# Two attention layers on one core: the first element's third item takes its denominators over memory and is scaled at the end; the projection's two blocks leave PSUM in one copy

## The chip, the core and the metric

One core of a Trainium2 chip runs the whole program. Its engines run side by side, each through its own queue in order: TensorE (PE; PEld is its loading of weights), VectorE (DVE), ScalarE (ACT), GpSimd (POOL), and SyncE (SP), which here only issues transfers. TensorE writes to PSUM, eight banks of 512 fp32 values in each of 128 partitions; ScalarE and VectorE read them from there. The metric is the device time of one execution in microseconds; the time given is the median of three runs.

## The reference

The input `x` has 16 elements (images) of 256 channels and 32 x 32 positions, all in fp32. Two layers follow each other. In the first, on the positions of an element as rows:

```
qkv  = x @ w_proj + b_proj                  # 4 heads of 64: q, k, v
attn = softmax(q @ k.T * 64**-0.5)
res  = attn @ v
x1   = res @ w_out + b_out + x
```

In the second, with a group norm `gn` over 32 groups of 8 channels:

```
q, k, v = gn(x1) @ qkv_w.T                  # 8 heads of 32
attn = softmax(q @ k.T * 32**-0.5 + phys_bias)
x2   = x1 + (attn @ v) @ proj_w.T + proj_b
out  = x2 + mlp_w2 @ gelu(mlp_w1 @ gn(x2) + mlp_b1) + mlp_b2
```

## The kernel before

**Layout.** Channels lie on the 128 partitions in `CC` = 2 chunks, the `S` = 1024 positions of an element in the free dimension, in `NT` = 2 blocks `t` of `TB` = 512. An element goes through two attentions, `attention_a` (first layer) and `attention_b` (second layer), and then the two-layer perceptron `mlp`. The elements `b` are run one after the other, but pieces of the perceptron of element b - 1 and of the query, key and value products of element b + 1 are put between the steps of an attention. The order of the program is written out by hand: the attentions are generators, a step being one block of keys (or two), and `later.after(n, fn)` runs `fn` n steps on. `tc.keep_in_program_order` and `tc.issue_after` set the order on one engine: what is traced inside `issue_after(ins)` stands behind `ins` in the queue of `ins`'s engine. Otherwise a scheduler orders the instructions of each engine when the program is built.

**The first attention.** `attention_a` works on four items, (t, c), two heads each. For each block `kb` of 128 keys the scores go to two PSUM banks (L434), ScalarE takes the exponential of the 128 x 1024 tile (L444), and `weigh` multiplies by the values (L457) and lets VectorE add the exponentials up over `kb` in `sums` (L471). At an item's last block the result leaves PSUM in two halves (L477, L478). The denominator of the softmax is the sum over keys: small matmuls with ones give it, repeated over the partitions (`den`). It is inverted in one of two ways. `denominators` (L375) copies it from PSUM (L376), lets SP spread the distinct values over all partitions (L381), inverts 16 values in each partition (L387), writes these to memory (L398) and reads them back repeated over the partitions (L403); GpSimd adds the values to two running totals from which the kernel later sees whether all denominators were in range. `normalise` does this for both items of a `t`, and `scale` multiplies. In element 0, for t = 1, `normalise_item` (L489) takes the other way: each item's denominator is inverted at full width on VectorE (L504, 128 x 512), the result multiplied (L505), and the range is kept with two reductions (L417). For item 2 (c = 0) ScalarE copies the denominator to SBUF first (L502) and this is done two steps after its end; for item 3 the reciprocal reads PSUM directly.

Behind the attention's last step stands the projection `o`: `project(0, res)` gives `first_half`, which is issued in two blocks of output channels, at L562 and L564; the part for t = 1 follows two steps after item 3. Two `o` blocks use PSUM banks `b0` and `b1`, and the two of the next `t` use the same.

**The second attention and its projection.** `attention_b` has four heads to a chunk and two blocks of keys to a step: scores (L602) into two single banks and three two-bank tiles, exponentials (L615), sums (L630), the values (L656). In elements 1 to 14 (`by_fold`) the sums of an item are folded to half height in a tile `packed_b`, kept in `spare["home"]`. When t = 0 is scaled, its projection `j` is issued in the course of the last item: `out_proj.issue` writes both blocks of 128 output channels to one two-bank tile `both` (L774), since `apart` is false there, and finds `home`. Then `leave(co)` runs for each block: ScalarE copies it to a quarter of `home` that is no longer needed and adds the bias on the way (L781), and one step later `add_up` adds it to the input and takes the statistics for the group norm on VectorE (L795, L796), behind the sums of that step. All other projections leave PSUM by one addition on VectorE that takes bias and input in (L787), with the statistics behind it (L790). The two banks of `both` are then taken by a score tile of the same step.

Of the kernel before, what the change touches and what calls it, by code (L numbers as in the profile page):

```python
# [10 lines left out]
AF = mybir.ActivationFunctionType  # L11
ALU = mybir.AluOpType
# [7 lines left out]
TB = 512  # L20
# [239 lines left out]
def first_pass(ctx, tc, x, out, k):  # L260
    nc = tc.nc
    B, C, S = x.shape
    CC, SB, NT = C // P, S // P, S // TB
    HC = k["m1b"].shape[1]
    later = Later()
# [44 lines left out]
    def wide(name, n=None):  # L310
        if n is None:
            n = next(m for m in order if m not in kept)
        use(n)
        return ps_s.tile([P, 2, TB], F32, tag=f"s{n}", name=name)

    def bank(name, n):
        return ps_a.tile([P, TB], F32, tag=f"b{n}", name=name)
# [36 lines left out]
    def product(o, w, r, **flags):  # L354
        for c0 in range(0, P, cols[0]):
            sl = slice(c0, c0 + cols[0])
            nc.tensor.matmul(o[sl], w[:, sl], r, **flags)  # L357
# [15 lines left out]
    spread_out, spare, trailing = {}, {}, []  # L373

    def denominators(key, den, d, full, waits, then, parts=1):  # L375
        nc.scalar.copy(d, den)  # L376
        n = full.shape[1]
        w = 4 * TB // P
        spread = work.tile([P, w], F32, tag="spread", name=f"sp_{key}", bufs=2)
        row = dram.tile([4 * TB // n, n], F32, tag="row", name=f"row_{key}", bufs=4)  # L380
        nc.sync.dma_start(  # L381
            spread, d[:: 32 // parts].rearrange("p (a b) -> p a b", b=w)
        )

        def invert():
            inverse = work.tile([P, w], F32, tag="inverse", name=f"inv_{key}", bufs=2)
            tc.keep_in_program_order(nc.vector.reciprocal(inverse, spread))  # L387
            if parts > 1:
                num = P // parts
                for r in range(parts):  # L390
                    nc.sync.dma_start(
                        row[:, r * n // parts : (r + 1) * n // parts].rearrange(
                            "g (a b) -> g a b", b=w
                        ),
                        inverse[r * num : (r + 1) * num],
                    )
            else:
                nc.sync.dma_start(row.rearrange("r (a b) -> (r a) b", b=w), inverse)  # L398
            nc.gpsimd.tensor_add(dsum, dsum, spread)
            nc.gpsimd.tensor_add(isum, isum, inverse)  # L400
            num = P * n // (4 * TB)
            for r in range(P // num):
                spread_out["last"] = nc.sync.dma_start(  # L403
                    full[r * num : (r + 1) * num], row[r].partition_broadcast(num)
                )
            later.after(waits[1], lambda: then(full))

        later.after(waits[0], invert)
# [5 lines left out]
    def add_to_range(den, inverse):  # L414
        for tot, what in ((dsum, den), (isum, inverse)):
            part = small.tile([P, 1], F32, tag="part", name="part")
            nc.vector.tensor_reduce(part, what, AX.X, ALU.add)  # L417
            nc.gpsimd.tensor_add(tot[:, :1], tot[:, :1], part)

    def attention_a(b, qT, kT, v, project):  # L420
        key, D, lag = f"a_{b}", D0, 2
        items = [(t, c) for t in range(NT) for c in range(CC)]
        units = [(i, kb) for i in range(len(items)) for kb in range(SB)]
        res = act.tile([P, CC, S], F32, tag="res", name=f"res_{key}")
        accs, held, sums, both, pair, homes = {}, {}, {}, {}, [], []
# [63 lines left out]
        def normalise_item(i):  # L489
            t, c = items[i]  # L490
            den = wide(f"den_{key}_{i}", next(m for m in order if m != 2))[:, 0, :]
            for j in range(4):
                nc.tensor.matmul(
                    den[j * 32 : (j + 1) * 32, :], k["ones"], sums[i][:, j // 2, :],
                    start=True, stop=True,
                )
            if not c:
                homes.append(act.tile([P, CC, S], F32, tag="k1", name=f"d_{key}_{t}"))
            full, held_den = homes[0][:, c, :TB], homes[0][:, c, TB:]
            r = res[:, c, t * TB : (t + 1) * TB]  # L500
            if c < CC - 1:
                nc.scalar.copy(held_den, den)  # L502
                den = held_den
            tc.keep_in_program_order(nc.vector.reciprocal(full, den))  # L504
            tc.keep_in_program_order(nc.vector.tensor_mul(r, r, full))  # L505
            if c == CC - 1:
                later.after(2, lambda: project(t, res)())
            later.after(3, lambda: add_to_range(den, full))

        def normalise(t):  # L510
            half = TB // 2
# [44 lines left out]
        while pending:  # L556
            weigh(*pending.pop(0))
            if not pending:


                first_half = project(0, res)
                first_half((0,), True)  # L562
                yield
                first_half((1,), True)  # L564
                cols[0] = P
                break
            yield
# [199 lines left out]
    def out_proj(key, w, src, bias, xs, t, stats, then):  # L767
        todo = list(range(CC))

        def issue(cos=range(CC), apart=False):  # L770
            home = None if apart else spare.pop("home", None)
            apart = apart or cols[0] == P
            if not apart:
                both = wide(f"{key}_{t}")  # L774
            ps = {}

            def leave(co):
                y = xs[:, co, t * TB : (t + 1) * TB]
                if home is not None:
                    held = home[:, 2 + co]  # L780
                    nc.scalar.activation(  # L781
                        held, ps[co], AF.Identity, bias=bias[:, co : co + 1]
                    )
                    later.after(1, lambda: add_up(co, y, held))
                    return
                else:
                    nc.vector.scalar_tensor_tensor(  # L787
                        y, ps[co], bias[:, co : co + 1], y, ALU.add, ALU.add
                    )
                nc.vector.bn_stats(stats[:, co, t, :], y)  # L790
                todo.remove(co)

            def add_up(co, y, held):
                with tc.issue_after(spread_out["es"].ins):
                    nc.vector.tensor_add(y, y, held)  # L795
                    nc.vector.bn_stats(stats[:, co, t, :], y)  # L796

            def part(co, kc):
                product(
                    ps[co],  # L800
                    w[:, kc, co * P : (co + 1) * P],
                    src(kc),
                    start=(kc == 0),
                    stop=(kc == CC - 1),
                )

            for co in cos:
                ps[co] = bank(f"{key}_{t}_{co}", co) if apart else both[:, co, :]
            if apart:
                for co in cos:  # L810
                    for kc in range(CC):
                        part(co, kc)
                    leave(co)
            else:
                for kc in range(CC):
                    for co in cos:
                        part(co, kc)
                for co in cos:
                    leave(co)
            if not todo and then:  # L820
                then()

        return issue
# [208 lines left out]
    def input_sums(key, y):  # L1032
        sums = weights_tile(f"qk7t_{key}")
        b11, b12 = (y[:, 0, t * TB : (t + 1) * TB] for t in range(NT))
        b21, b22 = (y[:, 1, t * TB : (t + 1) * TB] for t in range(NT))
        t1, t2, t3, t4 = (sums[:, n] for n in range(4))
        nc.vector.tensor_sub(t3, b22, b12)
        nc.vector.tensor_sub(t1, b12, b11)
        nc.vector.tensor_sub(t2, b22, t1)
        nc.vector.tensor_sub(t4, b21, t2)  # L1040
        return dict(t1=t1, t2=t2, t3=t3, t4=t4, b11=b11, b21=b21, b22=b22)
# [295 lines left out]
    ps, n = bank("bqk", 0), brow.shape[0]  # L1337
# [44 lines left out]
    for b in range(B):  # L1382
        def load_next(b=b):
# [3 lines left out]
            with tc.issue_after(spread_out["last"].ins):  # L1387
                load_blocks(1, b - 1)
                if b + 1 < B:
# [9 lines left out]
                lambda st, b=b, xn=xn, seven=seven, sums_1=sums_1: group_norm(  # L1399
                    f"g{b}", xs[b], st, k["g1w"], k["g1b"], "res", xn, 2 if b else 1,  # L1400
                    (lambda y: sums_1.update(input_sums(f"b{b}", y))) if seven else None,
                ),
# [62 lines left out]
        if first:  # L1465
# [10 lines left out]
                lambda st, b=b, hn=hn: group_norm(  # L1476
                    f"h{b}", xs[b], st, k["g2w"], k["g2b"], "q1", hn,
                    *((3 if b + 1 < B else 1), lambda y, b=b: sums_of_input(b, y)),
                ),
# [305 lines left out]
```

## Time and profile before

| | us |
|---|---|
| median of three runs | 3605.08 |
| lowest and highest | 3604.25, 3606.47 |
| the profiled execution | 3603.56 |
| its span, first to last instruction | 3601.8 |
| granted TensorE clock | 1.0 of full |

| group | count | mean ns | busy us |
|---|---|---|---|
| L504 full-width reciprocal, items 2 and 3 of element 0 | 2 | 3352 | 6.7 |
| L781 ScalarE copy with bias, 128 x 512 | 28 | 683 | 17.7 |
| L444 exponential, 128 x 1024 | 512 | 1024 | 520.7 |
| L795 VectorE addition, 128 x 512 | 28 | 682 | 19.1 |
| L787 addition with bias from PSUM, 128 x 512 | 100 | 744 | 74.2 |

A line of the profile names engine, source line, operation and tiles (written <- read). In a timeline the first two numbers are start and duration in microseconds, x is the number of instructions merged, and the bracket gives the idle time before them and what ended it. In a list of waits the three numbers are the total, how often, and the longest. Shares of busy time are averages; what a change is worth is read at the place where it works. Matmuls packed into parts of the array run side by side, so their number and duration say less than the distance from one group's start to the next.

### The profile page before, as it was taken

The numbers are of one execution on the slowest core, as the hardware profiler recorded it, in microseconds if no ns is written. First come the engines' busy times: TensorE is split into PE (matmuls) and PEld (weight loads), VectorE is DVE, ScalarE is ACT, GpSimd is POOL, SyncE is SP. The second block draws the span as 40 slices with busy tenths as digits, with TensorE's granted clock in tenths as the row PEclk, the third lists the DMA queues.
The fourth block names the chain that finished last, engine by engine and source line by source line (L and its number), as shares of the span: only waits on it lengthen the run. The fifth ranks groups of instructions, "written<-read, shape, count | busy, mean of one in ns | idle before, by whom it ended". The sixth has DMA issues, their size and how long they took to land.

```text
span 3601.8 us, 81991 instructions
## 1 busy us (share of the span) xinstructions
PE 3584.2 (100%) x35705; PEld 1470.2 (41%) x35705; DVE 2786.2 (77%) x3187; ACT 2283.0 (63%) x3196; POOL 219.1 (6%) x319
## 2 busy tenths in 40 slices
PE   9999999999999999999999999999999999999999
PEld 3334344343444434444344443434434444343433
DVE  5786877868788687876868878688786977868777
ACT  4665757667475675856658566585665757657572
POOL 4000100001000010000000000000000000000000
PEclk9999999999999999999999999999999999999999
DMA  3011311213122131221312213121121212213100
GB/s 130 8 57 33 78 54 38 74 38 83 45 43 69 39 81 45 50 64 36 81 45 52 66 33 81 45 55 63 39 76 45 55 63 47 74 39 64 51 28 28
DMA packets 81137, 197.78 MB, mean 55 GB/s; under 512 B 37666, under 2 KB 38434, under 8 KB 74626
## 3 DMA queue, kind: packets, MB, share of 16 engines
q1 hardware_dynamic: 71392, 163.85, 14.9%
q0 software_dynamic: 7632, 28.21, 5.1%
q8 instruction: 282, 4.62, 0.5%
q14 instruction: 85, 0.70, 0.1%
q10 hardware_dynamic: 1746, 0.40, 0.1%
HBM read 125.32 MB, written 22.27 MB: 41 GB/s over the span
## 4 chain that ended last, share of the span: by engine, by line
PE 92%; DVE 4%; issue 2%; DMA 1%; SPq 1%; ACT 1%; DVEq 0%; POOL 0%
PE s_b L602 12%; PE s_a L434 12%; PE acc_a L457 12%; PE acc_b L656 11%; PE m L357 10%; PE m L1146 10%; PE qk_b L1052 4%; PE qk_a L1052 3%; PE v_b L357 3%; PE j L357 3%; PE v_a L357 3%; PE o L357 3%; PE qk7y_b L1052 1%; PE qk7y_a L1052 1%; DVE es_b L630 1%
## 5 line engine op out<-in xcount | busy, mean ns | idle before, releaser
L615 ACT ACTIVATE e_b<-s_b 128x1024 f32<-128x1024 f32 (+1 forms) x1280 | 981.8, 865 | 135.6 <-PE s_b L602 135.6
L630 DVE TENSOR_TENSOR es_b<-es_b,e_b 128x2048 f32<-128x2048 f32 (+1 forms) x460 | 881.5, 1934 | 104.7 <-ACT e_b L615 88.3
L444 ACT ACTIVATE e_a<-s_a 128x1024 f32<-128x1024 f32 x512 | 520.7, 1024 | 360.3 <-PE s_a L434 359.6
L434 PE MATMUL s_a<-q,k 64*64 64x512 f32 x4096 | 544.5, 593 | 0.7 <-DVE res_a L478 0.7
L457 PE MATMUL acc_a<-e_a,v 64*64 64x512 f32 x4096 | 540.3, 589 | 0.0
L602 PE MATMUL s_b<-q,k 32*64 32x512 f32 x8192 | 527.1, 600 | 2.7 <-ACT v L928 1.3
L471 DVE TENSOR_TENSOR es_a<-es_a,e_a 128x1024 f32<-128x1024 f32 x384 | 469.8, 1224 | 66.0 <-ACT e_a L444 46.5
L656 PE MATMUL acc_b<-e_b,v 128*32 128x512 f32 x4096 | 492.2, 598 | 0.0
L357 PE MATMUL m<-g,w 128*32 128x256 f32 (+2 forms) x6464 | 416.6, 385 | 0.0
L357 PEld LDWEIGHTS m<-g,w 128*32 128x32 f32 (+1 forms) x6464 | 224.7, 111 | 212.0 <-issue 61.8
L457 PEld LDWEIGHTS acc_a<-e_a,v 64*64 64x64 f32 x4096 | 188.2, 133 | 251.2 <-issue 214.9
L602 PEld LDWEIGHTS s_b<-q,k 32*64 32x64 f32 x8192 | 175.9, 130 | 251.0 <-issue 133.0
L434 PEld LDWEIGHTS s_a<-q,k 64*64 64x64 f32 x4096 | 176.0, 133 | 247.5 <-issue 208.1
L656 PEld LDWEIGHTS acc_b<-e_b,v 128*32 128x32 f32 x4096 | 108.5, 109 | 351.5 <-ACT e_b L615 194.7
L630 DVE TENSOR_TENSOR es_b<-e_b,e_b 128x2048 f32<-128x2048 f32 (+1 forms) x72 | 147.0, 2051 | 131.2 <-ACT e_b L615 131.2
L1146 PE MATMUL m<-gn_h,w 128*128 128x512 f32 x512 | 242.5, 602 | 2.7 <-DVE x L1267 1.3
L1210 DVE TENSOR_TENSOR g<-g,g 128x512 f32<-128x512 f32 (+1 forms) x185 | 195.5, 1067 | 1.2 <-PE m L357 0.8
L1146 PE MATMUL m<-hs,w 128*128 128x512 f32 x384 | 178.2, 593 | 0.1
L1161 ACT ACTIVATE g<-g,m1b 128x512 f32<-128x512 f32 x128 | 91.8, 720 | 112.4 <-DVE g L1190 84.5
L1146 PEld LDWEIGHTS m<-gn_h,w 128*128 128x128 f32 x512 | 93.1, 190 | 118.7 <-issue 100.0
L1161 ACT ACTIVATE g<-m,m1b 128x512 f32<-128x512 f32 x128 | 80.9, 683 | 79.0 <-PE m L1146 79.0
L357 PE MATMUL v_a<-wp,x 128*32 128x256 f32 (+1 forms) x1952 | 121.7, 379 | 0.0
(225 smaller groups left out, 3527.9 us busy)
## 6 DMA issues: line engine op xcount, KB each, us to landing
w<-w_kept SPq DMA_DIRECT2D x30, 1792.0 KB
packed_b<-es_b SPq DMA_DIRECT2D x42, 512.0 KB
packed_b<-es_b POOLq DMA_DIRECT2D x42, 512.0 KB, 6.2
rd_b<-row_b SPq DMA_DIRECT2D x252, 64.0 KB
out_dram<-x SPq DMA_DIRECT2D x63, 256.0 KB
d_a<-row_a SPq DMA_DIRECT2D x62, 256.0 KB
x<-in_x_dram SPq DMA_DIRECT2D x30, 512.0 KB
qk<-qk_kept SPq DMA_DIRECT2D x14, 1024.0 KB
```

Source lines behind the costliest of these rows:

```text
L357: nc.tensor.matmul(o[sl], w[:, sl], r, **flags)
L434: nc.tensor.matmul(s[h : h + HALF, g, :], kT[g * D : (g + 1) * D, c, kb * P + h : kb * P + h + HALF], qT[g * D : (g + 1) * D, c, t * TB : ...
L444: nc.scalar.activation(e, s, AF.Exp, scale=float(D) ** -0.5)
L457: nc.tensor.matmul(accs[i][h][g * D : (g + 1) * D, :], v[h * HALF : (h + 1) * HALF, kb, c * 2 + g], e[h * HALF : (h + 1) * HALF, g, :], st ...
L471: spread_out["es"] = nc.vector.tensor_add(sums[i], held[i] if kb == 1 else sums[i], e)
L602: nc.tensor.matmul(outs[g][h : h + HALF, :], kT[g * D : (g + 1) * D, c, k0 : k0 + HALF], qT[g * D : (g + 1) * D, c, t * TB : (t + 1) * TB] ...
L615: spread_out["exp"] = nc.scalar.activation(to, s, AF.Exp, scale=float(D) ** -0.5)
L630: ins = nc.vector.tensor_add(d, (d if kb else es[0][:, g : g + step]), es[m][:, g : g + step])
L656: nc.tensor.matmul(acc[g * D : (g + 1) * D, :], v[:, kb + m, c * G + g], es[m][:, g, :], start=(m == 0), stop=(m == 1),)
L1052: nc.tensor.matmul(to, w, x[right], start=first, stop=True, skip_group_check=not first)
L1146: nc.tensor.matmul(ps, blocks[1][number - 1][:, i * P : (i + 1) * P], inputs[b][number], start=first, stop=True, skip_group_check=not first,)
L1210: (nc.vector.tensor_add if plus else nc.vector.tensor_sub)(d, d, more)
```

## The change

Part one concerns element 0, t = 1. Item 2 no longer gets its full-width reciprocal: `normalise_item` calls `denominators`, which takes the same trip over memory as the other blocks, into `homes[0][:, 0, :TB]`, and its product isn't taken there. The product moves to item 3's call, where the loop first multiplies item 2 by its inverse, then takes item 3's reciprocal and multiplies that. The last product is kept as `spread_out["scaled"]`; the VectorE instructions of `first_half` and of the reductions for item 3's range are put behind it. The range of item 2 goes the way of `denominators`, by GpSimd.

Part two concerns the projection `j` of t = 0 in elements 1 to 14. ScalarE takes both blocks from PSUM in one copy of 128 x 1024 without the bias, and `add_up` now does what `leave` does elsewhere, for both blocks: an addition on VectorE that takes in bias and input, and the statistics. Its inputs lie in SBUF.

In the compiled program TensorE issues the same matmuls; in element 0 one query-and-key matmul for element 1 stands before the second half of `o` instead of behind it, and one that stood behind the second statistics matmul stands before it. From element 1 on no engine's order changes but for the replaced instructions, and SP has six transfers more in element 0.

```diff
             full, held_den = homes[0][:, c, :TB], homes[0][:, c, TB:]
-            r = res[:, c, t * TB : (t + 1) * TB]
             if c < CC - 1:
-                nc.scalar.copy(held_den, den)
-                den = held_den
-            tc.keep_in_program_order(nc.vector.reciprocal(full, den))
-            tc.keep_in_program_order(nc.vector.tensor_mul(r, r, full))
-            if c == CC - 1:
-                later.after(2, lambda: project(t, res)())
-            later.after(3, lambda: add_to_range(den, full))
+                denominators(f"{key}_{i}", den, held_den, full, (2, 3), lambda full: None)
+                return
+            for m in range(CC):
+                r = res[:, m, t * TB : (t + 1) * TB]
+                if m == c:
+                    tc.keep_in_program_order(nc.vector.reciprocal(full, den))
+                scaled = tc.keep_in_program_order(
+                    nc.vector.tensor_mul(r, r, homes[0][:, m, :TB])
+                )
+            spread_out["scaled"] = scaled
+            later.after(2, lambda: project(t, res)())
+
+            def to_range():
+                with tc.issue_after(scaled.ins):
+                    add_to_range(den, full)
+
+            later.after(3, to_range)
...
                 first_half = project(0, res)
-                first_half((0,), True)
+
+                def part(co):
+                    if b:
+                        return first_half((co,), True)
+                    with tc.issue_after(spread_out["scaled"].ins):
+                        first_half((co,), True)
+
+                part(0)
                 yield
-                first_half((1,), True)
+                part(1)
...
-            def leave(co):
+            def leave(co, held=None):
                 y = xs[:, co, t * TB : (t + 1) * TB]
-                if home is not None:
-                    held = home[:, 2 + co]
-                    nc.scalar.activation(
-                        held, ps[co], AF.Identity, bias=bias[:, co : co + 1]
-                    )
-                    later.after(1, lambda: add_up(co, y, held))
-                    return
-                else:
-                    nc.vector.scalar_tensor_tensor(
-                        y, ps[co], bias[:, co : co + 1], y, ALU.add, ALU.add
-                    )
+                nc.vector.scalar_tensor_tensor(
+                    y, ps[co] if held is None else held[:, co], bias[:, co : co + 1], y,
+                    ALU.add, ALU.add,
+                )
                 nc.vector.bn_stats(stats[:, co, t, :], y)
-                todo.remove(co)
-
-            def add_up(co, y, held):
+                if held is None:
+                    todo.remove(co)
+
+            def add_up(held):
                 with tc.issue_after(spread_out["es"].ins):
-                    nc.vector.tensor_add(y, y, held)
-                    nc.vector.bn_stats(stats[:, co, t, :], y)
+                    for co in range(CC):
+                        leave(co, held)
...
-                for co in cos:
-                    leave(co)
+                if home is not None:
+                    held = home[:, 2:4]
+                    nc.scalar.copy(held, both)
+                    later.after(1, lambda: add_up(held))
+                else:
+                    for co in cos:
+                        leave(co)
```

## The prediction

> **What bounds the kernel now.** I read the page's busy times first, then TensorE's waits, then timelines of the places that the change touches. Busy times and waits:
>
> ```profile
> span 3601.8 us, 81991 instructions
> PE 3584.2 (100%) x35705; PEld 1470.2 (41%) x35705; DVE 2786.2 (77%) x3187; ACT 2283.0 (63%) x3196; POOL 219.1 (6%) x319
> ...
> PE den_a L493 <- DVE es_a L471: 2.6, 1, 2.6
> PE o L357 <- DVE res_a L541: 1.5, 2, 0.8
> PE warm L345 <- DVE nothing L1330: 1.5, 1, 1.5
> ```
>
> TensorE is idle for only 3601.8 - 3584.2 = 17.6 us in the whole span, so only what shortens a wait of TensorE can shorten the kernel, and no more than those waits. The longest one happens once: `den_a` of L493 stands 2.6 us behind VectorE's sums. It belongs to the first element's last item. VectorE's timeline there:
>
> ```profile
> 76.44 1.22 DVE L471 TENSOR_TENSOR es_a<-es_a,e_a 128x1024 f32<-128x1024 f32 x1
> 77.57 3.35 DVE L504 RECIPROCAL d_a<-d_a 128x512 f32<-128x512 f32 x1
> 80.83 1.16 DVE L471 TENSOR_TENSOR es_a<-es_a,e_a 128x1024 f32<-128x1024 f32 x1
> 81.91 0.68 DVE L505 TENSOR_TENSOR res_a<-res_a,d_a 128x512 f32<-128x512 f32 x1
> 82.51 1.27 DVE L417 TENSOR_REDUCE part<-d_a 128x1 f32<-128x512 f32 x2
> 83.69 5.20 DVE L471 TENSOR_TENSOR es_a<-es_a,e_a 128x1024 f32<-128x1024 f32 x4
> 88.82 0.68 DVE L478 TENSOR_TENSOR res_a<-res_a,acc_a 128x512 f32<-128x512 f32 x1
> 90.17 3.36 DVE L504 RECIPROCAL d_a<-den_a 128x512 f32<-128x512 f32 x1 [0.67 <-PE den_a L493]
> ```
>
> A full-width reciprocal (3.35 us), a product and two reductions of item 2 sit among the sums of item 3, and the sums end at 88.89, though their last exponential ended at 84.98 (ScalarE: 83.96 plus 1.02).
>
> A busy TensorE can also hide a loss, since packed matmuls can run half filled. In each element from 1 to 14 there is one such place, after `j`, the projection of the second attention:
>
> ```profile
> 414.90 1.98 PE L602 MATMUL s_b<-q,k 32*64 32x512 f32 x32
> 416.80 1.92 PE L656 MATMUL acc_b<-e_b,v 128*32 128x512 f32 x16
> 418.54 3.67 PE L357 MATMUL j<-res_b,wpj 128*32 128x512 f32 x32
> 422.15 2.54 PE L602 MATMUL s_b<-q,k 32*64 32x512 f32 x32
> 424.62 1.93 PE L656 MATMUL acc_b<-e_b,v 128*32 128x512 f32 x16
> ```
>
> The same 32 matmuls take 416.80 - 414.90 = 1.90 us up to the next group before `j`, and 424.62 - 422.15 = 2.47 us after it: 0.57 us lost with no idle time shown. I compared all starts of this block: the 0.57 is there in all 14 elements. ScalarE and the tile's own view say why:
>
> ```profile
> 422.29 1.26 ACT L781 ACTIVATE packed_b<-j,pjb 128x512 f32<-128x512 f32 x2 [1.96 <-PE j L357]
> 423.44 3.83 ACT L615 ACTIVATE e_b<-s_b 128x512 f32<-128x512 f32 x5
> ...
> who waited for it (us, times):
>   PEld s_b L602: 0.4, 1
> ```
>
> The last score tile of the block takes the two PSUM banks that `j` occupied. ScalarE frees them with its second copy, which ends at 423.551; the last eight matmuls start at 423.604.
>
> **What the Trainium skill says.** "Advanced Engine Details and Errata", The Read-Write Bubble: the latency of the memories shows between instructions, and "TRN2 allows reading multiple PSUM banks with single instruction". The trace agrees: L444 reads 1024 wide in 1024 ns, while two 512-wide L781 take 1.26 us. "VectorE: DVE Perf Modes", The TRN2 errata, gives ScalarE reading PSUM 172 cycles plus one for each element at 1.2 GHz: an estimate of 997 ns for 1024 elements and 570 for 512; the trace has 582 for the 512-wide copy of L477. "TensorE: Matmul & The Clock Gate", The mechanism, calls matmuls strictly first in, first out. This trace doesn't agree for packed ones: each fp32 matmul runs twice. In an undisturbed block eight tiles start their first passes within 50 ns and their second passes 0.48 us later, while at 157.92 us one tile ran both passes (157.917 and 158.396) before the seven behind it, held up, began at 159.062. "DMA: Bandwidth & Descriptors", Anatomy of one DMA, puts the fixed cost of a transfer at about 2 us, mostly the receipt of the write. The trace has 1.39 us for a row written and 2.05 for it read back, at 150.25 and 153.00.
>
> **Part one, element 0, item 2.** Removed from VectorE before the last sums: reciprocal 80.83 - 77.57 = 3.26, product 81.91 to 82.51 = 0.60, two reductions 82.51 to 83.69 = 1.18, together 5.04 us. Added: one 128x16 reciprocal (L387, 0.25). The sums then follow the exponentials, whose ends are 78.12, 79.89, 81.55, 83.33 and 84.98; a sum starts some 0.05 us after its exponential and takes 1.22, so the last ends at 86.25. TensorE's own work before `den_a` allows a start at about 86.4 (89.05 less the 2.58 of idle, less the change of shape). VectorE's end plus the 0.13 us seen before (88.89 to 89.02) gives 86.4 too. So the wait goes: **-2.6 us**.
>
> New is a round trip through memory. ScalarE's copy ends at 77.18 as before. SP spreads it (0.70) and it lands 2.0 us after the copy's end (in item 0: 60.99 to 63.07), at 79.25. The small reciprocal stands on VectorE behind the second sum (to 79.4) and ends near 79.65, before the third sum's exponential at 79.89, so it delays nothing. The row's write, SP's four issues and the landing took 150.22 to 155.05 = 4.83 us in the same form in the second attention, so `d_a` lands at 84.5. SP has nothing else between 67.3 and 142.3 us, and its queue runs empty there. GpSimd's two additions replace two others of about 0.2 to 0.7 us, with nothing behind them until 103.
>
> The product of item 2 moves behind the last L478. It waits for `d_a` at the head of VectorE's in-order queue, and behind it stand the last reciprocal, its product and the evacuation of both `o` banks, for which the second half of `o` waits. L478 ends at 87.9 (ScalarE's copy ends at 87.12). With `d_a` there at 84.5 there are 3.4 us to spare. Then: product to 88.5, reciprocal to 91.8, product to 92.4, first evacuation of `o` to 93.0. The compiled order gives TensorE, from 86.4: `den_a` 0.86, `o` 3.57, then three key-and-query matmuls instead of two: 2.57 plus the changes of shape, to 93.5. So the delayed evacuations are hidden by that third matmul with 0.4 us to spare; the statistics end at about 99.3 against 99.5 of TensorE. After the second statistics matmul one matmul less is left as cover: three are 2.6 us, and normalisation delivered its first block 2.54 us after it before. Cost nothing, up to 0.3 if either margin is off. Bounds: -2.7 to -1.3.
>
> **Part two, elements 1 to 14.** Two 512-wide copies become one of 1024. The trace has no such copy; L444's exponential of that shape takes 1024 ns, the page's estimate is 997, L615's back-to-back ones 1046. I take 1.02. It starts at 422.29 as before, because the first copy already waited for all of `j`. It ends at 423.31 instead of 423.55, the eight matmuls start 0.24 earlier, and so does all that follows: 14 x 0.24 = **-3.4 us**. If these matmuls had to queue behind the other tiles' second passes (423.488 to 423.508), only 0.10 to 0.12 would be gained, 14 x 0.11 = -1.6. If the whole gap closed, -8.0.
>
> VectorE's two additions (682 ns) become additions with a bias. Rows of that operation with one input in PSUM stand at 742 to 748; with both in SBUF there is none. I take 0.74, between 0.68 (nothing) and 1.4 (two passes). At 0.06 x 2 it adds 0.12 us an element. Behind them stands L674, which ends at 434.32 and frees the bank that `acc_a` takes at 435.57; 1.25 us cover it, 1.0 after TensorE's advance. Cost nothing. Nothing is late next in the element: `den_b` at 431.97 needs sums that ended at 430.6.
>
> **Sum.** -2.6 - 3.4 = -6.0 us on the profiled execution's 3603.56 (its span is 3601.8, 1.8 lie around it) gives 3597.6. The median of the runs shown is 3605.08, 1.5 above it; on that scale **3599.1 us**, 0.17% less. A measurement of this kernel can tell about 0.2% (7.2 us) from no change, so the forecast lies just inside that bound.
>
> **Rivals.**
> The eight matmuls queue in order, or the copy takes 1.1 us or more: -2.6 - 1.6 = -4.2, 3600.9. For it the skill's FIFO sentence; against it the block at 157.92.
> `d_a` comes late and the stall moves from `den_a` to the second half of `o`: every microsecond after 88.3 costs one. Under load in element 1 the trip took 8.7 us (277.6 to 286.3), which would land at 88.3, still free. With 1.5 us more, -1.1 - 3.4 = -4.5, 3600.6; against it DMA engines that are idle at 80 to 90 us (share 0.01).
> The gap of 0.57 closes whole: -2.6 - 8.0 = -10.6, 3594.5. It would need a copy of some 0.75 us, which no row of ScalarE shows.
> Slower than before: VectorE's biased addition from SBUF is the cost. In all 14 elements two of them hold up L674 and so `acc_a`. Each grown by x costs 2x - 1.0 an element; that outweighs 6.0 from x = 0.72, 1.4 us apiece. At 1.6 us: 14 x (1.84 - 1.01) = 11.6 lost, 3610.7. Only the missing row speaks for it; PSUM inputs don't slow the plain addition (682 in both).
>
> **How the numbers follow.** Forecast 0.57, in-order or slow copy 0.16, late `d_a` 0.10, whole gap 0.12, slower 0.05. The forecast's own spread is about 1.5 us (runs differ by 2.2, and VectorE-to-DMA stalls of 0.2 to 1 us in single elements shift), so about a quarter of it lies beyond 0.2%, that is below 3597.9. With the whole-gap case, faster has 0.27; slower has 0.03; the rest, 0.70, is within. The range 3595.5 to 3602.8 takes in the two smaller gains and the edge of the larger one.
>
> **What would show it.** L493's wait gone from TensorE's waits; the product of item 2 without a wait on DMA; the block after `j` 2.3 us long instead of 2.54; its copy at 1.02 us; the biased addition near 0.74. The prediction is wrong if that block stays at 2.54 or falls to 1.98, or if `o` waits for VectorE in element 0.

## The result and the profile after

The changed kernel takes 3599.01 us (median of 22 runs, 3598.42 to 3601.0), the kernel before 3605.25 in the same comparison (22 runs, 3602.95 to 3607.34): the ratio is 0.9984, 95% interval 0.9978 to 0.999. That is 6.2 us less (0.17%), clear of noise, where 6.0 were forecast.

The page of the changed kernel, its span and its busy times, then the head of TensorE's list of waits:

```profile
span 3597.1 us, 81973 instructions
...
PE 3580.9 (100%) x35705; PEld 1468.9 (41%) x35705; DVE 2783.7 (77%) x3185; ACT 2280.5 (63%) x3182; POOL 217.0 (6%) x319
```

```profile
PE j L357 <- DVE res_b L753: 1.6, 3, 0.7
PE warm L345 <- DVE nothing L1345: 1.5, 1, 1.5
PE m L1161 <- DVE x L1282: 1.3, 1, 1.3
PE o L357 <- DVE res_a L550: 1.3, 3, 0.7
```

`den_a`, the longest single wait before (2.6 us), is gone from the list. TensorE's busy time fell too, by 3.3 us (from 3584.2). Lines moved: the full-width reciprocal L504 is now L506, the product L505 is L508, the copy L781 is L830, VectorE's addition keeps the number L795 with the bias in it, and L674 is L690.

Element 0, VectorE's timeline after (start, duration, in brackets the idle time before), in which everything starts 0.16 us later than in the trace before:

```profile
79.46 0.24 DVE L387 RECIPROCAL inv_a<-sp_a 128x16 f32<-128x16 f32 x1
...
85.18 1.22 DVE L471 TENSOR_TENSOR es_a<-es_a,e_a 128x1024 f32<-128x1024 f32 x1 [0.43 <-ACT e_a L444]
87.32 0.69 DVE L478 TENSOR_TENSOR res_a<-res_a,acc_a 128x512 f32<-128x512 f32 x1 [0.91 <-ACT res_a L477]
87.92 0.68 DVE L508 TENSOR_TENSOR res_a<-res_a,d_a 128x512 f32<-128x512 f32 x1
88.52 3.35 DVE L506 RECIPROCAL d_a<-den_a 128x512 f32<-128x512 f32 x1
```

and TensorE's timeline of the same stretch:

```profile
86.56 1.06 PE L493 MATMUL den_a<-es_a,ones 128*32 128x512 f32 x8
...
90.99 2.84 PE L357 MATMUL qk_a<-x,wp 128*128 128x512 f32 x6
93.67 3.60 PE L357 MATMUL o<-res_a,wo 128*128 128x512 f32 x8
```

The sums follow their exponentials with gaps between them; the product of item 2 (L508 at 87.92) has no bracket, so VectorE stood idle for no DMA before it; the second half of `o` stands right behind the third query-and-key matmul, also without one. `den_a` starts at 86.56 instead of 89.05, 2.5 us earlier (2.6 with the later start).

Elements 1 to 14, the two changed groups (after the count: busy us, mean ns, then the idle time ahead of them):

```profile
L830 ACT COPY packed_b<-j 128x1024 f32<-128x1024 f32 x14 | 14.2, 1012 | 29.6 <-PE j L357 27.7 <-DVE es_b L646 1.9
L795 DVE SCALAR_TENSOR_TENSOR x<-packed_b,pjb,x 128x512 f32<-128x512 f32 x28 | 20.9, 745 | 0.0
```

TensorE's timeline at the place shown of before:

```profile
419.43 2.29 PE L618 MATMUL s_b<-q,k 32*64 32x512 f32 x32
421.65 1.92 PE L672 MATMUL acc_b<-e_b,v 128*32 128x512 f32 x16
```

and ScalarE's:

```profile
419.56 1.01 ACT L830 COPY packed_b<-j 128x1024 f32<-128x1024 f32 x1 [2.13 <-PE j L357]
420.55 3.84 ACT L631 ACTIVATE e_b<-s_b 128x512 f32<-128x512 f32 x5
```

From the start of the score block to the next group it is 421.65 - 419.43 = 2.22 us, against 2.47 before and 1.90 in an undisturbed block. The same 2.22 is found in all 14 elements. (The prediction and the expectations often give the group's own length instead, 2.54 or 1.98 us, which is 0.07 to 0.08 us more than this distance.)

### The profile page after: what moved, and what is told of

Same layout as the page of the kernel before. It is cut to its first block, busy times and chain, and to the rows that moved or that the text cites. A ratio compares the mean times of both kernels' runs of the same rounds, so it can differ in the third digit from the quotient of the medians.

```text
span 3597.1 us, 81973 instructions
## 1 busy us (share of the span) xinstructions
PE 3580.9 (100%) x35705; PEld 1468.9 (41%) x35705; DVE 2783.7 (77%) x3185; ACT 2280.5 (63%) x3182; POOL 217.0 (6%) x319
## 4 chain that ended last, share of the span: by engine, by line
PE 91%; DVE 5%; issue 2%; DMA 2%; SPq 1%; ACT 0%; DVEq 0%; POOL 0%
PE s_a L434 12%; PE acc_a L457 12%; PE s_b L618 12%; PE acc_b L672 11%; PE m L1161 10%; PE m L357 9%; PE qk_b L1067 4%; PE qk_a L1067 3%; PE v_b L357 3%; PE j L357 3%; PE o L357 3%; PE v_a L357 3%; DVE es_b L646 2%; PE qk7y_b L1067 1%; PE qk7y_a L1067 1%
## 5 line engine op out<-in xcount | busy, mean ns | idle before, releaser
L444 ACT ACTIVATE e_a<-s_a 128x1024 f32<-128x1024 f32 x512 | 520.7, 1024 | 360.3 <-PE s_a L434 360.3
```

The costliest lines, as they stand in the source:

```text
L444: nc.scalar.activation(e, s, AF.Exp, scale=float(D) ** -0.5)
```

## The experiments

What each kernel took, against the kernel before on the same chip; the fourth column is the distance just explained, the same to 0.02 us in all 14 elements of a kernel. The median of before differs from chip to chip (3603.74 to 3605.25), so two kernels that ran on different chips are compared by the third column, and by their traces:

| kernel | median us | minus before | block after j, us |
|---|---|---|---|
| before | | | 2.47 |
| changed | 3599.01 | -6.2 | 2.22 |
| p1_only | 3600.07 | -3.7 | 2.47 |
| p2_only | 3601.33 | -2.4 | 2.22 |
| two_copies | 3597.62 | -6.1 | 2.28 |
| early | 3618.90 | +15.2 | 1.90, but j is cut in two |
| own_bank | 3605.30 | +1.1 | 2.67 |
| own_bank_bias | 3606.97 | +2.7 | 2.77 |
| own_bank_swap | 3593.99 | -10.5 | 1.90 |
| own_bank_swap_bias | 3594.65 | -9.1 | 1.91 |
| dve4 | 3617.11 | +12.6 | 2.22 |
| defer_only, late6, dve1 (one run each) | 3599.78, 3601.31, 3600.63 | -4.5, -2.9, -3.8 | 2.22 |

### Each part alone

p1_only is the change without its edits to `out_proj`; p2_only has those alone. The diffs are the halves of the diff above.

> Part one alone (the memory trip and the late product in element 0; the copies of elements 1 to 14 stay as before: two of 512 with their bias on ScalarE). The theory of the prediction: TensorE's wait of den_a for VectorE's sums in element 0 (2.6 us) is gone and nothing takes its place, so 2.6 us less than before, about 3602.6; the block of score matmuls after j stays at 2.54 us. Rival (the two parts help each other, or the gain of element 0 is eaten by later waits of TensorE for VectorE or a DMA): the wait is gone but the time is within 1 us of before.

> Part two alone (one 1024-wide copy in elements 1 to 14, bias added on VectorE; element 0 as before). The theory: the block after j is 0.24 us shorter in each of 14 elements, so 3.4 us less than before, about 3601.8; the 2.6 us wait of den_a is still there. Rival (the irregular waits of j for the scaled second attention give half of it back): 1.5 to 2 us less. Both parts' gains should add up to that of the whole change, 6.2 us.

Ratios 0.999 (0.9983 to 0.9997) and 0.9994 (0.9986 to 1.0002): part two alone is not clear of noise. The intervals are 2.5 to 2.9 us wide to either side, so these times alone can't tell 2.6 from 3.7 or 2.4 from 3.4. The traces can tell what each part does at its place. In p1_only the wait of `den_a` is gone and the block after `j` is 2.47 as before. In p2_only the block is 2.22 everywhere and its list of waits still has the old head:

```profile
PE den_a L493 <- DVE es_a L471: 2.6, 1, 2.6
```

The two gains, 3.7 and 2.4, add up to 6.1, against 6.2 of the whole, but each is 1.0 to 1.1 us from what its place shows (2.6 and 3.5). Other waits of TensorE scatter. One is that of `j` for the scaled result of the second attention (L737 before, L753 in the changed kernel), which waits for a DMA. Summed as the excess of `j`'s distance to the next group over its undisturbed 3.55 us, it is 1.5 us in the profiled execution of before, 2.2 in p1_only, 2.4 in p2_only and 3.1 after. Another is that of `o` for the scaled result of the first attention: 1.5, 0.7, 0.9 and 1.3 us in the lists of waits. In p2_only's profile `j` so takes 0.9 of the 3.5 us back, as its rival says, and the span is 2.9 us shorter. In p1_only's profile the span is 3.4 us shorter, more than the 2.6, since `o` and a few smaller waits lost less. In the profiles of before and after the spans differ by 3601.8 - 3597.1 = 4.7, some 1.5 less than the medians do, about what `j` lost more (1.6). Whether `j`'s waits grow because TensorE arrives earlier, or only differ from one execution to the next, one profile of each kernel can't tell.

### One copy, or no bias?

two_copies changes one line of the changed kernel:

```diff
-                    nc.scalar.copy(held, both)
+                    for co in cos:
+                        nc.scalar.copy(held[:, co], both[:, co])
```

> The changed kernel, but ScalarE takes the two blocks of the projection in two plain 512-wide copies; the bias stays on VectorE. It tells what of part two's gain comes from the single copy and what from taking the bias off ScalarE. If the bias was the cost: the first copy takes 0.58 us instead of 0.68, the second ends 1.07 us after the start of the first (against 1.26 before and 1.01 in the changed kernel), and the block after j is 2.35 us long: 14 x 0.19 = 2.7 of the 3.5 us stay, some 0.8 us above the changed kernel. If the single instruction was it (a fixed cost for each instruction or its wait): 1.2 us and more, the block at 2.5, 3 us above the changed kernel.

ScalarE's timeline of this run:

```profile
419.42 1.07 ACT L831 COPY packed_b<-j 128x512 f32<-128x512 f32 x2 [2.14 <-PE j L357]
```

1.07 us for the two, as worked out, and a block of 2.28 (2.35 in the expectation's measure). Of the 0.25 us won in an element, 2.47 - 2.28 = 0.19 come from taking the bias off ScalarE (0.09 a copy: 683 ns before, 589 plain here), and 0.06 from making one instruction of two. The ratio, 0.9982 (0.9976 to 0.9989), can't be told from that of the change: the 0.8 us between them are less than these times resolve.

### Where TensorE's remaining loss is, and a kernel without it

In the changed kernel 0.32 us are still lost after `j` in each of 14 elements. early tries to free a bank sooner by finishing the first block of `j` first:

```diff
-                for kc in range(CC):
-                    for co in cos:
-                        part(co, kc)
                 if home is not None:
                     held = home[:, 2:4]
-                    nc.scalar.copy(held, both)
+                    for co in cos:
+                        for kc in range(CC):
+                            part(co, kc)
+                        nc.scalar.copy(held[:, co], both[:, co])
...
                 else:
+                    for kc in range(CC):
+                        for co in cos:
+                            part(co, kc)
```

> The changed kernel, but the projection's 32 matmuls in elements 1 to 14 run output block by output block, and ScalarE copies each block (plain, 512 wide) with a wait of its own, as soon as that block is done. If the rest of the gap after j (0.32 us in each of 14 elements) is only the copy that TensorE waits for, the first copy moves beside the second half of j, one copy of 0.58 us stands after j, and the block after j is 1.98 us long: 14 x 0.32 = 4.5 us less than the changed kernel, about 3594.5. If the dependency is kept for the whole tile, or TensorE's writes into one bank hold up the reading of the other, nothing is gained: within 1 us of the variant with two plain copies. If the other order of j's matmuls packs worse, j itself grows from 3.6 us by some tenths, and it is slower than the changed kernel.

None of the three: the ratio is 1.0044 (1.003 to 1.0058). TensorE's timeline of the run:

```profile
415.63 1.04 PE L357 MATMUL j<-res_b,wpj 128*32 128x512 f32 x8
417.45 1.07 PE L357 MATMUL j<-res_b,wpj 128*32 128x512 f32 x8 [0.78 <-DVE res_b L753]
418.45 1.07 PE L618 MATMUL s_b<-q,k 32*64 32x512 f32 x2
419.45 1.92 PE L357 MATMUL j<-res_b,wpj 128*32 128x512 f32 x16
421.30 1.97 PE L618 MATMUL s_b<-q,k 32*64 32x512 f32 x30
```

and a line of the list of waits of its weight loads (total, times, longest):

```profile
PEld j L357 <- ACT packed_b L830: 11.4, 14, 0.8
```

The block after `j` is short at last (421.30 to 423.20), but `j` itself pays twice. Its second block waits for the copy of the first, 0.8 us in each element: the two lie in one tile, and the program makes the one wait for the other though they are in different banks. In two_copies likewise the first copy starts only after all of `j`, though its own block was done before. And its ninth matmul record already needs the later half of `res_b`, 0.86 us sooner than in the old order; those waits on L753 grow to 8.3 us (1.6 in the changed kernel). From `j` to the end of the score block it is 102.9 us in 14 elements, against 83.8 in the changed kernel.

So TensorE's order has to stay, and the blocks of `j` need tiles of their own. own_bank puts the second one into bank `b1`; own_bank_bias is the same edit on top of p1_only:

```diff
+            halves = {} if apart or home is None else {0: both[:, 0, :], 1: bank(f"{key}_{t}_1", 1)}
...
-                ps[co] = bank(f"{key}_{t}_{co}", co) if apart else both[:, co, :]
+                ps[co] = bank(f"{key}_{t}_{co}", co) if apart else halves.get(co, both[:, co, :])
...
-                    nc.scalar.copy(held, both)
+                    for co in cos:
+                        nc.scalar.copy(held[:, co], ps[co])
```

> The changed kernel, but in elements 1 to 14 the second block of j goes to a PSUM bank of its own (b1, free there until den_b), so that the first block's copy no longer has to wait for all of j, and the last score tile only for that first copy; two plain 512-wide copies, TensorE's order unchanged. Theory (the 0.32 us that are still lost after j are TensorE waiting for the copy and nothing else): ScalarE's first copy runs beside the last quarter of j, the block after j takes 1.90 us up to the next group as elsewhere, 14 x 0.32 = 4.5 us less than the changed kernel, about 10.7 less than before. Rival (the loss is a cost of changing from one shape of matmul to the other after j, which a copy cannot take away): no gain over the changed kernel. Rival (the bank is not free: den_b or its neighbour then waits for the second copy): the block is short, but a new wait at den_b gives it back.

> Part one of the change, and instead of its part two the bank of its own for the second block of j, with the two biased 512-wide copies on ScalarE and the plain additions on VectorE as before. Theory: once the copy that frees the banks of the last score tile is not the last work after j, its length no longer matters: the same time as the variant with plain copies, within 1 us. Rival (the bias on ScalarE costs somewhere else too, since each copy is 0.1 us longer and the exponentials come behind it): about 2.7 us above it.

My premise was wrong: `b1` is not free until `den_b`. The score step after `j` uses both single banks first and its two-bank tiles last, so `b1` holds its second score tile. TensorE's timeline in own_bank:

```profile
418.90 2.74 PE L618 MATMUL s_b<-q,k 32*64 32x512 f32 x32
421.57 1.92 PE L672 MATMUL acc_b<-e_b,v 128*32 128x512 f32 x16
```

and ScalarE's:

```profile
418.18 0.59 ACT L832 COPY packed_b<-j 128x512 f32<-128x512 f32 x1 [1.12 <-PE j L357]
419.04 0.59 ACT L832 COPY packed_b<-j 128x512 f32<-128x512 f32 x1 [0.27 <-PE j L357]
```

The first copy now does run beside the last quarter of `j`. But the block starts at 418.90, its third matmul wants `b1` at once, and the second copy holds it to 419.63; the trace has that matmul at 419.68. The five matmuls behind it begin right after it (419.69 to 419.72), though in own_bank_swap below they begin within 0.05 us of the block's start: a matmul that is held up holds those behind it too. The wait has moved from the last score tile to the second: 0.77 us instead of 0.32, and the ratio is 1.0004 (0.9996 to 1.0012), no gain at all. With the bias it is 0.1 us longer (2.77), so own_bank_bias missed its expectation for the same reason: there a copy is what TensorE waits for. The run own_bank_swap exchanges the two:

```diff
-            ... {0: both[:, 0, :], 1: bank(f"{key}_{t}_1", 1)}
+            ... {0: bank(f"{key}_{t}_0", 1), 1: both[:, 0, :]}
```

> The run with the bank of its own, with the two blocks of j exchanged: its first block, done 0.86 us before the second, goes to bank b1, which the second score tile after j takes, and the second block goes to the shared pair, which the last score tile takes. From the run before: the copies end 0.25 us before and 0.60 us after the end of j's last start to next start, so the second score tile (wanted 0.03 us after the block's start) finds b1 free, and the last one (wanted 1.4 us after it) finds its pair free. Theory (TensorE's loss after j is its wait for ScalarE's copies and only that): the block is 1.90 us up to the next group, 14 x 0.32 = 4.5 us less than the changed kernel, about 10.7 less than before. Rival (a cost of the change of shape after j): the block stays at 2.2 us and the time at that of the changed kernel.

TensorE's timeline of this run:

```profile
419.22 1.97 PE L618 MATMUL s_b<-q,k 32*64 32x512 f32 x32
421.12 1.92 PE L672 MATMUL acc_b<-e_b,v 128*32 128x512 f32 x16
```

and ScalarE's:

```profile
418.50 0.59 ACT L832 COPY packed_b<-j 128x512 f32<-128x512 f32 x1 [1.20 <-PE j L357]
419.35 0.58 ACT L832 COPY packed_b<-j 128x512 f32<-128x512 f32 x1 [0.27 <-PE j L357]
```

The first copy ends at 419.08, before the block starts, the second at 419.94, before the last tile is wanted at 420.6. The block is 421.12 - 419.22 = 1.90 us in all 14 elements, and the kernel takes 3593.99 us, ratio 0.9971 (0.996 to 0.9983): faster than before. That it is faster than the change too rests on the block and on the spans (3592.1 against 3597.1), since the two ratios' intervals overlap a little. There was no cost of the change of shape in that gap, only the wait.

The run own_bank_swap_bias takes part two of the change back in this arrangement; it is the same edit on top of p1_only:

> The run with exchanged banks, but with part two of the change undone: ScalarE's two copies carry the bias (0.68 us each instead of 0.58), VectorE adds without it. In the run before, the first copy ended at 419.08 and the second score tile started at 419.22, the second ended at 419.94 and the last score tile started at 420.55 to 420.58. With 0.1 us more each, the copies end at 419.18 and 420.04: still ahead. Theory (the length of the copies counts only where TensorE waits for the copy): the block stays at 1.90 us, and the time within 1 us of the run with exchanged banks. Rival (the bias on ScalarE costs wherever it stands): 14 x 0.2 = 2.8 us more.

The block is 1.91 us, 0.01 longer, and the span 3592.2 against 3592.1; the ratio is 0.9974 (0.9965 to 0.9984). On the medians the gain is 1.4 us smaller (9.1 against 10.5, on two chips), outside the expected 1 us but well inside the intervals, so the answer rests on the block: where TensorE doesn't wait for the copy, the bias on ScalarE costs next to nothing (14 x 0.012 = 0.2 us of the rival's 2.8).

### The trip through memory

defer_only undoes the trip alone:

```diff
-                denominators(f"{key}_{i}", den, held_den, full, (2, 3), lambda full: None)
+                nc.scalar.copy(held_den, den)
+                tc.keep_in_program_order(nc.vector.reciprocal(full, held_den))
```

> The changed kernel, but item 2 of element 0 keeps its full-width reciprocal among the sums (no trip through memory); only its product is late. The two range reductions of item 2's denominators are left out. It tells what of the 2.6 us is owed to the trip and what to moving the product and the reductions. From the timeline of before: after the reciprocal (to 80.9) five sums follow back to back at up to 1.3 us each, so they end near 87.3 instead of 86.3 and den_a waits for them 0.8 us (between 0.3 and 0.9): most of the gain, 1.8 of 2.6, comes without the trip. Rival (only the removed reciprocal frees VectorE in time): the wait stays near 2.6 less the 0.6 of the product.

VectorE's timeline of this run:

```profile
77.84 3.34 DVE L502 RECIPROCAL d_a<-d_a 128x512 f32<-128x512 f32 x1
81.11 6.48 DVE L471 TENSOR_TENSOR es_a<-es_a,e_a 128x1024 f32<-128x1024 f32 x5
```

and TensorE's:

```profile
87.73 1.06 PE L493 MATMUL den_a<-es_a,ones 128*32 128x512 f32 x8 [0.99 <-DVE es_a L471]
```

1.0 us of waiting is left, a little over my bound of 0.9: the five sums take the full 1.3 us apiece and end at 87.59. So, in this order of steps, 1.6 of the 2.6 us come from moving the product and leaving out the reductions, and 1.0 from the trip. (These are waits read from the trace; a single run's time can't tell such amounts.)

late6 starts the trip later, with 6 in place of 2 for the step at which the small reciprocal is issued:

> The changed kernel, but the small reciprocal of item 2's denominators in element 0 stands four steps later, behind the first of the last two sums: it ends near 84.9 instead of 79.7, so the row's trip starts 5.2 us later. The prediction had d_a land at 84.5 (84.7 on the clock of this trace) with 3.4 us to spare before the product. If that slack was right, d_a lands at 89.9, the product waits 2.0 us for the DMA, and the second half of o, which had 0.4 us in hand, waits for VectorE about 1.6 us. If the trip is longer than worked out (6 us), the wait is 2.8 us; if shorter (4 us), 0.8 us. If the trip never mattered there, TensorE shows no wait.

VectorE's timeline of this run:

```profile
85.05 0.25 DVE L387 RECIPROCAL inv_a<-sp_a 128x16 f32<-128x16 f32 x1
...
90.45 0.69 DVE L508 TENSOR_TENSOR res_a<-res_a,d_a 128x512 f32<-128x512 f32 x1 [2.06 <-DMA d_a<-row_a]
```

and TensorE's:

```profile
95.86 3.70 PE L357 MATMUL o<-res_a,wo 128*128 128x512 f32 x8 [1.64 <-DVE x L795]
```

The product waits 2.06 us and `o` 1.64, as worked out. From the end of the small reciprocal (85.30) to the product it is 5.15 us; put behind 79.70 in the changed kernel, that is a landing near 84.9, some 3 us ahead of the product. And 2.06 - 1.64 = 0.42 us is what TensorE has in hand at `o`.

### VectorE's cover

dve4 and dve1 add n operations behind the biased additions, n = 4 and 1:

```diff
                     for co in range(CC):
                         leave(co, held)
+                    for m in range(n):
+                        r = held[:, m % CC]
+                        nc.vector.tensor_tensor(r, r, r, op=ALU.max)
```

> The changed kernel with four more VectorE operations of 128x512 (the maximum of packed_b's held block with itself, which changes no value) behind the two biased additions in each of elements 1 to 14: 4 x 0.61 = 2.4 us more before L690, which frees the bank that acc_a takes. In the changed kernel L690 ends at 431.70 and acc_a starts at 432.59. Theory of the prediction (VectorE's additions have about 1 us of cover, and what goes beyond it holds up acc_a): 2.4 - 0.9 = 1.5 us an element, 14 x 1.5 = 21 us more than the changed kernel. Rival (VectorE is idle enough, 77% busy, so nothing waits for it): within 1 us of the changed kernel.

> The same with one more VectorE operation (0.61 us): inside the cover of 0.9 us, so no wait of acc_a and no more time than the irregular waits make from run to run, within 1.5 us of the changed kernel. If there is no such cover and every microsecond of VectorE there counts: 14 x 0.6 = 8.5 us more.

The place in the changed kernel, on VectorE and on TensorE:

```profile
431.03 0.67 DVE L690 TENSOR_TENSOR room_b<-room_b,acc_b 128x512 f32<-128x512 f32 x1
```

```profile
432.59 1.04 PE L457 MATMUL acc_a<-e_a,v 64*64 64x512 f32 x8
```

L690 ends 0.9 us before `acc_a` starts. dve4 takes 3617.11 us, ratio 1.0034 (1.002 to 1.0047), 18 us above the changed kernel (18.9 by the third column of the table). Its list of waits is headed by:

```profile
PE acc_a L457 <- DVE room_b L690: 13.3, 12, 1.4
PE acc_a L457 <- ACT e_a L444: 2.7, 2, 1.3
```

From the start of the first score tiles of `s_a` to `acc_a` it is 4.1 to 4.2 us in nine elements instead of 2.63, the 1.5 of the expectation; in the other five it is 3.3 to 4.0, and why is left open. Added up over the 14 elements that is 18.4 us more, as measured. In dve1 it is 2.63 in all 14: nothing waits there. The 1.6 us that this single run lies above the changed kernel (2.4 by the third column), outside the expected 1.5, are lost elsewhere: in its trace the first `v_a` of element 0 starts at 22.23 us instead of 20.25, behind a wait of 1.5 us of `qk_a` for ScalarE, long before the first added operation.

## Why the prediction was right

**Part one, -2.6.** The trace has 2.6 at its place. The path was the one given: reciprocal, product and reductions out from among the sums, the sums behind their exponentials. The cover held too: `d_a` was to have 3.4 us to spare, late6 puts it at about 3; the second half of `o` was to have 0.4 us in hand, late6 shows 0.42. Nothing was given back behind `o`: `qk_b` starts at 103.70 against 106.18.

**Part two, -3.4.** 14 x (2.47 - 2.22) = 3.5. The copy takes 1.01 us (1.02 taken), the biased addition 745 ns (740 taken). The 0.24 was one term in the prediction, which compared the single copy with two copies that also carried the bias, 1.26 us. two_copies splits it into 0.19 for the bias and 0.06 for the single instruction: the size was right, but most of it comes from the bias and not from the single copy.

The rival that lets the matmuls queue in order would have left a block of 2.35 or 2.36 us. In the trace after, the copy ends at 420.58 and the four matmuls that waited for it start their first passes at 420.63, ahead of the second passes of the four before them at 420.77. So this rival is out, but the prediction read too much into the block at 157.92. What interleaves is the two passes of a matmul (each leaves two records in the trace). At 157.92 the first matmul ran both passes while the others were held up, which no more breaks their order than own_bank does, where a held matmul holds all behind it. Nothing read here shows a later matmul beginning before an earlier one.

Of the 4.7 us between the two spans, 3.3 came off TensorE's busy time. The prediction's sentence that no more than the 17.6 us of idle time can be won was therefore too narrow, as its own next step, the loss hidden in busy time, already implies.

**The slower rival.** Its place and its price are real, only its size is not. The cover before `acc_a` was put at 1.0 us after the advance; the profile after has L690's end at 431.70 and `acc_a` at 432.59, 0.9. 0.6 us more on VectorE makes nothing wait there (dve1), 2.4 us more cost 18 in all (dve4). A biased addition of 0.745 us is far from that.

**The whole-gap rival.** It did not come with this change, and for the reason given: the copy of 1024 took 1.01 us, not 0.75. What the prediction did not see is that the copy need not be short if half of it starts earlier and each bank is given to the tile that needs it at the right time: own_bank_swap closes the gap, 14 x 0.32 = 4.5 us, and measures 4.2 us more gain than the change (10.48 against 6.24, each against before on its own chip).

**The sum.** -6.0 forecast, -6.2 measured, with an interval of -7.9 to -3.6: it includes the forecast, but also the smaller gains of two rivals. What rules these out are the traces, not the time. That forecast and median agree to 0.2 us is luck in part: the irregular waits of `j` alone differ by 1.6 us between the profiles of before and after, and the two parts alone measured 3.7 and 2.4 where 2.6 and 3.4 were forecast, misses that cancel in the sum.

## What to carry to other kernels

A busy TensorE can hide a wait: compare the distance between starts of the same group at different places, and where one is longer, look for the engine that frees its PSUM banks. There, shorten the instruction that ends last (a bias moved to an engine with slack), or better, let the bank that is finished first go to the tile that is wanted first, so that the copy is no longer last. And before an edit is costed at nothing, work out the time that covers it: the margins read from the trace here (0.4, 0.9 and about 3 us) fit what the experiments cost when they went beyond them, but for the five elements of dve4 that lost less.

## What the runs showed of the hardware

ScalarE's 512-wide copy from PSUM takes 0.09 us more with a bias for each partition than without (683 ns in before, 589 in two_copies), while two plain ones in a row take only 0.06 us more than one of 1024 (1.07 against 1.01). On VectorE an addition with a bias takes 745 ns against 682 without, whether its input lies in SBUF (745) or in PSUM (744).
